# The walk over a strip of eight image columns in the scan's sums into yacc

## The chip, the cores and the metric

The kernel runs on one core of a Trainium2 chip. The metric is the device time of one execution in microseconds (us). Before the change it is 24400.92 us, the median of three runs (24385.79 to 24407.32).

The engines' names in profile lines: PE is TensorE (PEld its weight loads), DVE VectorE, ACT ScalarE, POOL GpSimd, SP SyncE, which here issues DMAs.

## What is computed

Eight images of 64 x 64 pixels and 192 channels go through two layers, each with a residual sum. Layer 0 is a Mamba-2 block between two depthwise convolutions. Layer 1, which the change is in, is a two-dimensional selective scan: four directions run over each image, along rows (k = 0), along columns (k = 1), and both backwards (k = 2 and 3). Their outputs are brought back to the order of rows and summed:

```python
xs = jnp.stack([x_flat, x_t], axis=1)                       # rows, columns
xs = jnp.concatenate([xs, jnp.flip(xs, axis=-1)], axis=1)   # and both backwards
...
dA = jnp.exp(d[..., None] * A[None])
dBu = (d * uu)[..., None] * bm[:, :, None, :]
hst = dA * hst + dBu
y = jnp.einsum('bkdn,bkn->bkd', hst, cm)
...
y = y1 + inv2 + wh + invwh      # wh, invwh: columns, transposed back to rows
```

384 inner channels and 16 states per channel take part. The sum `y` is then normalised over the channels, multiplied with a gate and projected back to 192 channels.

## The kernel before

Layer 0 runs first over all images, then layer 1 image by image. In layer 1 an image has a front stage (projection, depthwise convolution, SiLU; it writes the convolved image to DRAM twice, in the order of rows and in that of columns), a scan stage, and a finishing stage that runs beside the front stage of the next image. Front and finish are ordered by a planner (`Flow`), which takes a weight per step. The scan stage is `main()`, whose order is written out by hand. The sums that the change is in are issued in `main()`, so none of the planner's weights belongs to them.

**The scan.** The 384 channels are three groups of 128 (`d`). One direction of 4096 positions is cut into 8 chunks of 512 (`TT`), so an image has 32 steps `(k, c)`. A step has 24 units: 8 pairs of states (`p`) times 3 groups (`d`). For each unit

- `decay` (L1569, ScalarE) makes exp(delta times A) for 2 x 512 elements,
- `weigh` (L1554, ScalarE) and `supply` (L1580, TensorE transposes) make the inputs of the recurrence in PSUM,
- `run` does two scans of 128 x 512 on VectorE (L1596), one small copy of the last state on GpSimd (L1608) and one product with C on GpSimd (L1610),
- `collect` (L1625, TensorE) sums the states into `y`, a PSUM tile of 128 x 512, one per group `d`; the 8 pairs accumulate into it,
- `add` (L1634 and L1636, VectorE) acts after the eighth pair alone: it adds the finished `y` to `yacc`, the SBUF buffer of 128 x 3 x 4096 in which the four directions meet. For k = 0 it is a copy (L1634), for k = 1, 2 and 3 a sum in place (L1636).

In the loop of `main()` the order on the engines is: `run(u)`, `decay(u + 2)`, some `weigh`, `supply(u + 1)`, `collect(u - 1)`, `add(u - 2)`, then pieces of the preparation of the next step. So the sum of a unit follows two iterations after that unit's `run`: a step's three sums stand in VectorE's queue in three successive iterations (its last one and the first two of the next step), each behind one unit's two scans and ahead of the next unit's. The preparation of a step has some VectorE work of its own (L1446, L1462, L1482, L1502).

**The views.** `yacc` holds each channel's image along rows, position 64 h + w. A chunk of a row direction is 8 rows, that is 512 adjacent words of `yacc`. A chunk of a column direction is 8 adjacent columns of 64 pixels. `y` holds it in the direction's own order, column by column (position 64 w + h within the chunk). `view` picks the chunk's place in `yacc`, and `seq` gives `y` the same order of dimensions. The two lines that matter are `rearrange("p (h w) -> p w h", ...)` in `view`, for yacc, and `rearrange("p (w h) -> p w h", ...)` in `seq`, for y. In both the innermost dimension is h: yacc is walked with a step of 64 words (256 bytes), as source and as destination, and y word after word.

Of the kernel before, what the change touches and what calls it, by code (L numbers as in the profile page):

```python
# [14 lines left out]
NB, HI, WI, C = 8, 64, 64, 192  # L15
# [1014 lines left out]
def layer1(tc, consts, x1s, mv1, out, w_in, w_x, w_dt, w_out):  # L1030
# [7 lines left out]
    with ExitStack() as ctx:  # L1038
# [352 lines left out]
        def view(buf, k, d, at, n):  # L1391

            if k % 2 == 0:
                return buf[:, d, at : at + n]
            return buf[:, d].rearrange("p (h w) -> p w h", w=WI)[:, at // HI : (at + n) // HI, :]

        def seq(ap, k):

            return ap if k % 2 == 0 else ap.rearrange("p (w h) -> p w h", h=HI)

        def scan(xo):

# [224 lines left out]
            def add(u):  # L1627
                s, p, d = units[u]
                k, c = steps[s]
                if p == NP1 - 1:  # L1630
                    ya = view(yacc, k, d, c * TT, TT)
                    yv = seq(state[s]["y", d], k)
                    if k == 0:
                        o(nc.vector.tensor_copy(ya, yv))  # L1634
                    else:
                        o(nc.vector.tensor_add(ya, ya, yv))  # L1636
# [218 lines left out]
```

## Time and profile before

| what | value |
|---|---|
| median of three runs | 24400.92 us |
| the profiled execution's own time | 24391.89 us |
| its span | 24390.1 us |
| TensorE clock granted, mean | 0.973 |
| VectorE busy | 21614.8 us (89%) |
| ScalarE busy | 21445.6 us (88%) |
| TensorE busy | 20962.6 us (86%) |
| GpSimd busy | 16900.2 us (69%) |
| chain of waits, largest shares | GpSimd 53%, TensorE 23% |
| L1634, copies of y into yacc | 192 of 665 ns |
| L1636, sums of y into yacc | 576, 625.5 us busy |

A line of the groups gives line, engine, operation, tiles and shapes, the count, then busy time and mean duration of one in ns, then the engine's idle time before such instructions and what ended it. A line of one source line's view gives the shortest, median and longest duration. A line of a stretch gives its bounds and length in us, then each engine's busy time with its count of instructions, the granted clock, the DMA share and the rate. A line of the timeline gives start, duration, engine, line and operation; a bracket at its end is idle time before it and what ended that.

From 4.8 ms or so on, layer 1 runs; the scans take most of it. Within it, each image's scan stage shows 32 steps of about 67 to 70 us.

### The profile page before, as it was taken

Reading aid. Unit: us, or ns where it says so; the run is one execution under the profiler, and the core shown is the slowest. Engines: PE = TensorE matmul, PEld = TensorE weight load, DVE = VectorE, ACT = ScalarE, POOL = GpSimd, SP = SyncE. Lnnn points to the kernel's source line nnn. Section 1 sums busy time; section 2 is a strip of 40 time slices with the busy share of each in tenths; the row PEclk is TensorE's granted clock in tenths of the full one; section 3 lists DMA queues with packets and bytes.
Section 4 is the critical chain, followed back from the end, with each engine's and each line's share of the span. In section 5 each row is a group of like instructions: output and inputs, shape, how many; then the busy total and the mean of one; then the engine's idle time right before and its main releaser. Section 6 shows DMA issues by size and latency. Waiting matters only on the chain.

```text
span 24390.1 us, 313055 instructions
## 1 busy us (share of the span) xinstructions
PE 20962.6 (86%) x100036; PEld 10175.2 (42%) x100036; DVE 21614.8 (89%) x22093; ACT 21445.6 (88%) x38076; POOL 16900.2 (69%) x13639
## 2 busy tenths in 40 slices
PE   7999999978888888888888888888888888888888
PEld 4444444434443444344434443444344334434444
DVE  7888888689988999899989998999899989998998
ACT  5666666589998999899889998998899899989998
POOL 1111111169976997799779977997799779977997
PEclk8999999989999999999999999999999999999999
DMA  2111111122222222222222222222222222222221
GB/s 49 44 43 45 46 44 46 39 84 66 67 68 85 66 67 70 84 66 67 71 81 67 67 75 79 65 67 74 81 65 67 73 81 67 67 71 81 66 67 56
DMA packets 1129702, 1608.05 MB, mean 66 GB/s; under 512 B 259360, under 2 KB 458432, under 8 KB 1118848
## 3 DMA queue, kind: packets, MB, share of 16 engines
q1 hardware_dynamic: 1128064, 1588.03, 23.0%
q8 instruction: 806, 13.21, 0.2%
q14 instruction: 832, 6.82, 0.1%
HBM read 1024.65 MB, written 160.17 MB: 49 GB/s over the span
## 4 chain that ended last, share of the span: by engine, by line
POOL 53%; PE 23%; issue 9%; DVE 7%; ACT 6%; DMA 1%; SPq 0%; POOLq 0%; DVEq 0%; ACTq 0%
POOL hc L1610 48%; POOL cy L1608 4%; PE p_f L953 3%; DVE xs L1200 2%; PE y L1625 2%; ACT pw L1554 2%; PE p_f L973 2%; ACT ea L1569 2%; PE p_x L445 2%; PE p_o L870 1%; POOL du L1489 1%; PE p_y L787 1%; PE p_z L528 1%; PE p_o L1374 1%; DMA xc<-xo 1%
## 5 line engine op out<-in xcount | busy, mean ns | idle before, releaser
L1610 POOL TENSOR_TENSOR hc<-hs,cb 128x1024 f32<-128x1024 f32 x6144 | 14597.2, 2376 | 9.8 <-POOL cy L1608 5.2
L1596 DVE TENSOR_TENSOR_SCAN hs<-ea,cy,g 128x512 f32<-128x512 f32 x10752 | 13061.1, 1263 | 785.6 <-PE g L1580 412.2
L1554 ACT ACTIVATE pw<-duT,bt 128x384 f32<-128x384 f32 x16384 | 8873.7, 601 | 12.2 <-DVE duT L1502 12.2
L1625 PE MATMUL y<-hc,sel 128*64 128x512 f32 x24576 | 6652.9, 620 | 2470.5 <-POOL hc L1610 2463.7
L1569 ACT ACTIVATE ea<-dr,an 128x512 f32<-128x512 f32 x12288 | 8125.8, 709 | 350.7 <-DVE hs L1596 328.5
L1580 PEld LDWEIGHTS g<-ident,pw 128*128 128x128 f32 x49152 | 5306.7, 141 | 4301.4 <-issue 2670.3
L1580 PE MATMUL g<-ident,pw 128*128 128x128 f32 x49152 | 6771.8, 280 | 30.0 <-DVE hs L1596 12.9
L1625 PEld LDWEIGHTS y<-hc,sel 128*64 128x64 f32 x24576 | 1228.7, 135 | 3889.7 <-POOL hc L1610 3629.3
L1608 POOL COPY cy<-hs 128x2 f32<-128x2 f32 x6144 | 1179.3, 192 | 1543.8 <-DVE hs L1596 1431.3
L1489 POOL TENSOR_TENSOR du<-de,xc 128x512 f32<-128x512 f32 x768 | 984.8, 1282 | 1636.4 <-DVE de L1482 1620.1
L1596 DVE TENSOR_TENSOR_SCAN hs<-ea,g 128x512 f32<-128x512 f32 x1536 | 1777.2, 1205 | 180.6 <-PE g L1580 125.8
L362 POOL TENSOR_TENSOR s<-xs 96x512 f32<-96x512 f32 x64 | 117.0, 1829 | 2035.0 <-DVE xs L340 1523.2
L1200 DVE SCALAR_TENSOR_TENSOR xs<-pad,p,xs 128x4096 f32<-128x4096 f32 x192 | 860.8, 4484 | 37.4 <-ACT xs L1190 30.2
L1468 PE MATMUL p_dt<-xdbl,wd 13*128 13x512 f32 x1536 | 856.8, 639 | 41.6 <-DVE de L1482 39.7
L362 POOL TENSOR_TENSOR s<-sq 96x512 f32<-96x512 f32 x128 | 206.7, 1615 | 965.4 <-ACT sq L375 890.2
L1439 PE MATMUL p_d<-xc,wx 128*44 128x512 f32 x1536 | 792.7, 598 | 96.3 <-DMA xc<-xo 96.3
L340 DVE SCALAR_TENSOR_TENSOR x<-xx,p,x 96x512 f32<-96x512 f32 x1024 | 784.8, 814 | 15.3 <-ACT x L329 15.3
L953 PE MATMUL p_f<-h,wf 96*128 96x512 f32 x1536 | 763.9, 633 | 24.4 <-ACT zs L547 14.0
L340 DVE SCALAR_TENSOR_TENSOR xs<-xin,p,xs 96x512 f32<-96x512 f32 x1024 | 749.8, 768 | 4.6 <-ACT xs L329 4.6
L1482 DVE SCALAR_TENSOR_TENSOR de<-p_dt,spa 128x512 f32<-128x512 f32 x768 | 524.2, 683 | 254.3 <-ACT spa L1477 253.5
L973 PE MATMUL p_f<-m,wf 128*96 128x512 f32 x1536 | 692.1, 601 | 0.0
L1636 DVE TENSOR_TENSOR yacc<-yacc,y 128x512 f32<-128x512 f32 x576 | 625.5, 1086 | 16.6 <-PE y L1625 16.6
(201 smaller groups left out, 19661.2 us busy)
## 6 DMA issues: line engine op xcount, KB each, us to landing
cb<-cd SPq DMA_DIRECT2D x4096, 128.0 KB
dr<-de SPq DMA_DIRECT2D x3072, 128.0 KB
xc<-xo SPq DMA_DIRECT2D x256, 768.0 KB
e<-csd SPq DMA_DIRECT2D x256, 384.0 KB
xl<-x SPq DMA_DIRECT2D x256, 384.0 KB
xo<-xs SPq DMA_DIRECT2D x48, 1024.0 KB
xo<-xt SPq DMA_DIRECT2D x24, 2048.0 KB
xl<-in_x SPq DMA_DIRECT2D x64, 384.0 KB
```

The source lines that it names most:

```text
L340: nc.vector.scalar_tensor_tensor(im(out[:, ct]), tap(ct, j), w[:, ct, j : j + 1], im(out[:, ct]), ALU.mult, ALU.add)
L953: nc.tensor.matmul(ps, wf1[:, ct, mt * 128 : mt * 128 + 128], h[:, ct], start=ct == 0, stop=ct == 1)
L973: nc.tensor.matmul(ps[:CP], wf2[:, kt, ct * CP : ct * CP + CP], m[:, kt], start=kt == 0, stop=kt == 5)
L1200: nc.vector.scalar_tensor_tensor(xs, tap(j), kw[:, d, j : j + 1], xs, ALU.mult, ALU.add)
L1489: o(nc.gpsimd.tensor_mul(st["du", d], st["de", d], st["xc"][:, d]))
L1554: nc.scalar.activation(st["pw", p, j][:, :, i], st["duT"][:, j].rearrange("p (g c) -> p g c", c=64), AF.Copy, scale=st["bt"][:, j, n : n + 1],
L1569: nc.scalar.activation(ea[:, f], state[s]["dr", d][:, f], AF.Exp, scale=an[:, k, p, at : at + 1])
L1580: nc.tensor.transpose(g[:, f, j * 128 : j * 128 + 128], state[s]["pw", p, j][:, 2 * d + f].rearrange("p a b -> p (a b)"), ident,)
L1596: nc.vector.tensor_tensor_scan(rev(h[:, f]), rev(ea[:, f]), rev(g[:, f]), 0.0 if first(s) else state[s - 1]["cy"][:, p, d, f : f + 1], ALU ...
L1608: o(nc.gpsimd.tensor_copy(st["cy"][:, p, d], h[:, :, last]))
L1610: o(nc.gpsimd.tensor_mul(hc, h, bc(st["cb", p], 1, [128, 2, TT])))
L1625: o(nc.tensor.matmul(y[half[f]], sel, hc[:, f], start=p == 0 and k > 0, stop=p == NP1 - 1))
```

## The change

Both views are turned, in the column directions alone: the innermost dimension is now w, of which a chunk has 8. yacc is walked along the rows of the strip, 8 adjacent words in each of 64 rows that lie 64 words apart, as source and destination. y, in PSUM, is read in the matching order: 8 words with a step of 64, then the next h. The same elements meet, each sum is one instruction of 512 elements per partition as before, and the row directions (k = 0 and 2) are untouched. Nothing else in the kernel differs.

```diff
             if k % 2 == 0:
                 return buf[:, d, at : at + n]
-            return buf[:, d].rearrange("p (h w) -> p w h", w=WI)[:, at // HI : (at + n) // HI, :]
+            return buf[:, d].rearrange("p (h w) -> p h w", w=WI)[:, :, at // HI : (at + n) // HI]
 
         def seq(ap, k):
 
-            return ap if k % 2 == 0 else ap.rearrange("p (w h) -> p w h", h=HI)
+            return ap if k % 2 == 0 else ap.rearrange("p (w h) -> p h w", h=HI)
```

## The prediction

> **What bounds the kernel now.** I read the groups of instructions first, for the price of the operation that is edited; then its own line; then stretches of the scan, one chunk long, to see whether that price reaches the end; then the engines' order of work inside such a stretch.
>
> ```profile
> L1596 DVE TENSOR_TENSOR_SCAN hs<-ea,cy,g 128x512 f32<-128x512 f32 x10752 | 13061.1, 1263 | 785.6 <-PE g L1580 412.2
> L1636 DVE TENSOR_TENSOR yacc<-yacc,y 128x512 f32<-128x512 f32 x576 | 625.5, 1086 | 16.6 <-PE y L1625 16.6
> ...
> L1636 DVE TENSOR_TENSOR yacc<-yacc,y x576: 657/1285/1358, 5656.5 to 24254.9; 128x512 f32<-128x512 f32 x192
> ```
>
> The sums into yacc (L1636) have one shape but two prices: 657 ns at least, 1285 ns in the median. Of the 576, 192 belong to direction 2 (rows) and 384 to directions 1 and 3 (columns). Sorted by direction with the Vector engine's timeline they take 662 ns (657 to 667) in direction 2, and 1300 and 1296 ns in directions 1 and 3: mean 1298 ns. Check: 192 x 0.662 + 384 x 1.298 = 625.5 us, the row's busy time. So the edit touches 384 instructions that each cost 0.636 us more than their row twin, 244 us of the Vector engine's time.
>
> Whether those 244 us are time of the kernel is seen by setting directions side by side. One chunk from the start of its first sum to that of the next chunk: lines one and two are direction 2, three and four direction 3. Both run backwards in time, with the same instructions, and differ in the view alone.
>
> ```profile
> core 0: us, PE busy (x) PEld busy (x) DVE busy (x) ACT busy (x) POOL busy (x), PEclk, DMA share, GB/s
> 16002.80:16070.45 67.65, 57.63 (x316) 28.49 (x316) 63.61 (x60) 66.97 (x122) 63.37 (x52) 1.00 0.23 69
> 16070.45:16138.11 67.66, 57.78 (x318) 28.46 (x316) 63.62 (x60) 67.27 (x122) 63.36 (x52) 1.00 0.24 67
> ...
> 16545.70:16615.18 69.48, 57.75 (x317) 28.48 (x316) 65.36 (x61) 67.45 (x122) 63.28 (x52) 1.00 0.22 62
> 16615.18:16684.68 69.50, 57.79 (x318) 28.50 (x316) 65.36 (x60) 67.47 (x122) 63.23 (x52) 1.00 0.25 69
> ```
>
> A row chunk takes 67.65 us and ScalarE (ACT) is busy 67.0 to 67.3 us of it: it is the floor there. A column chunk takes 69.5 us, ScalarE works no more than before and is idle for 2 us, and the Vector engine (DVE) has 1.75 us more to do. The place is seen in the order of its work, first direction 2, then direction 3:
>
> ```profile
> 16002.80 0.66 DVE L1636 TENSOR_TENSOR yacc<-yacc,y 128x512 f32<-128x512 f32 x1
> 16003.38 2.44 DVE L1596 TENSOR_TENSOR_SCAN hs<-ea,cy,g 128x512 f32<-128x512 f32 x2
> 16005.74 0.66 DVE L1636 TENSOR_TENSOR yacc<-yacc,y 128x512 f32<-128x512 f32 x1
> ...
> 16545.70 1.28 DVE L1636 TENSOR_TENSOR yacc<-yacc,y 128x512 f32<-128x512 f32 x1
> 16546.89 2.46 DVE L1596 TENSOR_TENSOR_SCAN hs<-ea,cy,g 128x512 f32<-128x512 f32 x2
> 16549.24 1.31 DVE L1636 TENSOR_TENSOR yacc<-yacc,y 128x512 f32<-128x512 f32 x1
> ```
>
> Around the three sums of a chunk the Vector engine has no idle time; sum to sum is 2.94 us in direction 2 and 3.54 us in direction 3. GpSimd (POOL) waits behind it there:
>
> ```profile
> 16549.41 0.19 POOL L1608 COPY cy<-hs 128x2 f32<-128x2 f32 x1 [0.99 <-DVE hs L1596]
> 16552.97 0.19 POOL L1608 COPY cy<-hs 128x2 f32<-128x2 f32 x1 [1.00 <-DVE hs L1596]
> ```
>
> The same waits are 0.37 to 0.43 us in direction 2. The chain of waits gives GpSimd 53% of the span, but in these microseconds it follows the scans, which stand in the Vector queue behind the sum. So a sum's length is on the path, and a row chunk is a model of what a column chunk becomes if its sums get as short.
>
> [...] One reading stream that hops is shown on ScalarE, by its column copy against a copy of the same size along rows:
>
> ```profile
> L1227 ACT COPY xt<-xs 128x4096 f32<-128x4096 f32 x24 | 176.3, 7346 | 0.3
> L1190 ACT ACTIVATE xs<-pad,p 128x4096 f32<-128x4096 f32 x24 | 91.1, 3794 | 0.2
> ```
>
> 7346 / 4096 = 1.79 ns per element against 0.93[...]. No instruction of this trace hops in PSUM.
>
> **The change part by part.**
> Removed: the hop of yacc, as source and destination, in 384 sums. After it yacc comes in runs of 8 adjacent words, 64 of them, each starting at a multiple of 32 bytes. [...] No row here has runs of 8; nothing hides this, it is priced at 0[...]. [...]
> Added: y, in PSUM, was read in order and is now read with a step of 64 words eight times, then from one word on. This decides. [...] I take 0, and keep both ends.
> Moved: nothing. The count of instructions, their order, the queues, the DMAs and the waits are the same; the sums aren't among the costs of the planner. Nothing new is queued behind them.
> Sum, for a sum of 0.662 us. Starts of first sums over the whole trace give these chunk times: direction 1, 69.55 us mean (56 chunks); direction 2, 67.73 (56); direction 3, 69.57 (48). Gains: 56 x (69.55 - 67.73) = 102 us; the last chunk of direction 1 against the last of direction 2, 8 x (68.74 - 66.99) = 14 us; direction 3, 56 x (69.57 - 67.73) = 103 us (the seventh of each image has no next chunk to prepare; I price it the same). The very last chunk's sums stand beside a Vector engine that waits for TensorE (idle 0.36 and 1.19 us before them), and the mean's matmul waits for the last for 0.3 us: 0.25 x 8 = 2 us. Together 221 us of the 244: 91% of a sum's saving reaches the end. The rest is chunk ends, and ScalarE's floor of 67.3 us, which is late next: below it a shorter sum would buy nothing.
> The profiled execution took 24391.9 us (span 24390.1 and 1.8 around it): 24391.9 - 221 = 24171. It was 9 us below the median of 24400.9, so the forecast in medians is **24180 us**, 0.9% faster. Per microsecond of a sum's length: 221 / 0.636 = 347 us.
>
> **The rivals.**
> *PSUM hops like SBUF.* [...] **24300**. [...] With 0.95 to 1.13 us, 24280 to 24342.
> *The stride only moves over.* [...] about **24400**. [...]
> *Slower.* [...] the Vector queue holds the scans longer than now. It decides from a sum of 1.298 + 49 / 347 = 1.44 us on[...] **24526**. [...]
> *ScalarE keeps the time.* It was busy 67.45 us in column chunks against 67.1 in row chunks; if that stayed, a chunk would take 67.45 + 0.6 = 68.05 us, the 112 chunks would gain 1.5 us each and the whole some 170 us: 24230. Equal counts (122) speak against it; it lies in the range.
>
> **Chances.** Free hop (with the ScalarE variant) 0.46; SBUF-like hop 0.34; moved over 0.12; slower 0.08. By the bound of 0.2% (49 us, about what a measurement of this kernel can tell from no change), the first two are faster: 0.80; the third is within: 0.12; 0.08 slower. The range is the first two: from 24155 (24180 less the 21 us by which the runs before spread, rounded) to 24340, where the SBUF-like case ends.
>
> **What would show it.** The line of L1636 has one price, 0.66 us for all 576, busy 381 us; chunks of directions 1 and 3 take 67.7 us like direction 2; sums follow at 2.94 us; GpSimd's copies wait 0.4 us. If the sums are 0.66 and the chunks are not 67.7, the path is wrong; if they take 1.0 us or more, the price of the PSUM hop is, and the time should follow at 347 us per microsecond.

## The result and the profile after

The changed kernel takes 24180.17 us (median of 5 runs, 24169.79 to 24198.37) where the kernel before takes 24407.32 us (5 runs, 24385.79 to 24414.17): a ratio of 0.9909, 95% interval 0.9895 to 0.9922. That is 227 us, or 0.9% less. The forecast was 24180 us.

The sums' own line of the profile after, and their group:

```profile
L1636 DVE TENSOR_TENSOR yacc<-yacc,y x576: 657/662/689, 5666.8 to 24042.8; 128x512 f32<-128x512 f32 x192
L1636 DVE TENSOR_TENSOR yacc<-yacc,y 128x512 f32<-128x512 f32 x576 | 382.0, 663 | 25.7 <-PE y L1625 25.7
```

There is one price now. 657 to 689 ns covers all three directions, and the busy time has fallen from 625.5 to 382.0 us. By direction the medians are 664, 662 and 662 ns for directions 1, 2 and 3: reading y with a step of 64 words in PSUM (directions 1 and 3) costs nothing that these records show beside the reading in order (direction 2, 662 ns).

Two stretches of direction 3 in the profile after, each one chunk long and beginning 0.28 us ahead of a chunk's first sum:

```profile
core 0: us, PE busy (x) PEld busy (x) DVE busy (x) ACT busy (x) POOL busy (x), PEclk, DMA share, GB/s
16430.84:16498.49 67.65, 57.77 (x318) 28.46 (x317) 63.62 (x60) 67.24 (x122) 63.29 (x52) 1.00 0.23 65
16498.49:16566.15 67.66, 57.80 (x318) 28.48 (x317) 63.63 (x60) 67.27 (x122) 63.34 (x52) 1.00 0.25 70
```

They take what the row chunks took before: 67.65 us, with 63.6 us of VectorE and 67.2 us of ScalarE. The order of work at the head of such a chunk, on VectorE and on GpSimd behind it:

```profile
16431.12 0.67 DVE L1636 TENSOR_TENSOR yacc<-yacc,y 128x512 f32<-128x512 f32 x1
16431.70 2.45 DVE L1596 TENSOR_TENSOR_SCAN hs<-ea,cy,g 128x512 f32<-128x512 f32 x2
16434.06 0.67 DVE L1636 TENSOR_TENSOR yacc<-yacc,y 128x512 f32<-128x512 f32 x1
...
16434.22 0.18 POOL L1608 COPY cy<-hs 128x2 f32<-128x2 f32 x1 [0.39 <-DVE hs L1596]
16437.16 0.19 POOL L1608 COPY cy<-hs 128x2 f32<-128x2 f32 x1 [0.39 <-DVE hs L1596]
```

The sums follow each other at 2.94 us, and GpSimd's copies wait 0.39 us instead of 1 us. The gain reaches the end through VectorE's queue, in which the next scan stands behind the sum: the trace before has hardly an instruction on another engine that waits for a sum itself (three waits, 0.9 us in all). ScalarE shows the same in its idle time. The first line is from the kernel before, from its groups:

```profile
L1569 ACT ACTIVATE ea<-dr,an 128x512 f32<-128x512 f32 x12288 | 8125.8, 709 | 350.7 <-DVE hs L1596 328.5
```

and this is the same group after:

```profile
L1569 ACT ACTIVATE ea<-dr,an 128x512 f32<-128x512 f32 x12288 | 8123.2, 709 | 159.9 <-DVE hs L1596 131.9
```

Its work is the same to 3 us. What it waited for VectorE's scans is down by 197 us.

Where the time went is seen best in the scan stages alone (first to last scan of each image, from the traces), because the rest differs from run to run: in kernels with the same layer 0, the first scan starts 5022 to 5051 us into the execution. The eight scan stages took 17535.9 us before and 17317.5 us after: 218.4 us less. The work between them is the same to a few us. One more trace of the changed kernel (run e7_after_again below) gives 17328.6 us: two traces of one kernel can differ by 11 us here.

### The profile page after: what moved, and what is told of

The parts are those of the page before. It is cut to its first block, busy times and chain, and to the rows that moved or that the text cites. A ratio compares the mean times of both kernels' runs of the same rounds, so it can differ in the third digit from the quotient of the medians.

```text
span 24174.9 us, 313055 instructions
## 1 busy us (share of the span) xinstructions
PE 20986.5 (87%) x100036; PEld 10182.8 (42%) x100036; DVE 21386.3 (88%) x22093; ACT 21415.5 (89%) x38076; POOL 16907.4 (70%) x13639
## 4 chain that ended last, share of the span: by engine, by line
POOL 53%; PE 25%; issue 8%; DVE 6%; ACT 5%; DMA 2%; SPq 1%; POOLq 0%; DVEq 0%; ACTq 0%
POOL hc L1610 47%; POOL cy L1608 4%; PE y L1625 3%; PE p_f L953 3%; DVE xs L1200 3%; PE p_f L973 2%; PE p_x L445 2%; PE g L1580 2%; ACT pw L1554 2%; DMA xc<-xo 2%; PE p_o L870 1%; POOL du L1489 1%; ACT ea L1569 1%; PE p_y L787 1%; PE p_d L1439 1%
## 5 line engine op out<-in xcount | busy, mean ns | idle before, releaser
L1482 DVE SCALAR_TENSOR_TENSOR de<-p_dt,spa 128x512 f32<-128x512 f32 x768 | 524.1, 682 | 254.0 <-ACT spa L1477 253.0
L1495 PEld LDWEIGHTS p_du<-ident,du 128*128 128x128 f32 x3072 | 323.1, 141 | 743.2 <-POOL du L1489 500.3
```

## Experiments

The theory: a stream that hops in SBUF lengthens the sum (1.298 us against 0.662 with two such streams, in the trace before), a stream that reads PSUM with hops does not (0.663 us after), and the time that a sum keeps VectorE from its next scan is time of the kernel, until ScalarE's work is the limit. "Hopping" means that the innermost step is more than one word. Each run is compared within itself: chunks of directions 1 and 3 against those of direction 2, which no run alters except where it is said. All runs start from the changed kernel.

**One hopping stream at a time.** The first kernel hops in the source alone, the second in the destination alone.

```diff
-                        o(nc.vector.tensor_add(ya, ya, yv))
+                        src = yacc[:, (d + 1) % DT].rearrange("p (h w) -> p w h", w=WI)[:, 8 * c : 8 * c + 8, :]
+                        dst = yacc[:, d, c * TT : c * TT + TT].rearrange("p (w h) -> p w h", h=HI)
+                        o(nc.vector.tensor_add(dst, src, state[s]["y", d].rearrange("p (w h) -> p w h", h=HI)))
```

(k = 2 keeps its sum; the second kernel exchanges the two views.)

> Leaves out the right place: in directions 1 and 3 the sum reads yacc down the columns of one channel group (step of 64 words) and writes 512 adjacent words of another, y is read in order; the output isn't the reference's. Theory ([...] PSUM has nothing to do with it): [...] at 347 us per us of a sum's length the kernel takes about 24300 us, half-way between after and before. Rival A (only hopping writes are dear, reads hop for nothing): 0.66 us and 24180. Rival B (only hopping reads are dear): 1.30 us and 24400.

> The mirror of the run with the hopping source: in directions 1 and 3 the sum reads 512 adjacent words of yacc in another channel group and writes down the columns (step of 64 words), y is read in order; the output isn't the reference's. Theory (both streams pay by themselves): 1.00 us per sum and about 24300 us. Rival A (only writes are dear): 1.30 us and 24400. Rival B (only reads are dear): 0.66 us and 24180.

Measured: 24298.77 us (ratio to before 0.9963, 0.9951 to 0.9976) with the hopping source and 24256.15 us (0.9951, 0.9938 to 0.9963) with the hopping destination. The sums take 1048 and 1053 ns: both streams pay, and rivals A and B fall. The times lie on either side of the half-way that had been expected of both (a ratio of 0.9955), the second kernel's 44 us below the 24300 named for it; the intervals of the two overlap, so it is their chunks that tell them apart. Equal durations gave unequal chunks. Timeline of VectorE in direction 3, source hopping:

```profile
16491.57 1.05 DVE L1640 TENSOR_TENSOR yacc<-yacc,y 128x512 f32<-128x512 f32 x1
16492.53 2.45 DVE L1596 TENSOR_TENSOR_SCAN hs<-ea,cy,g 128x512 f32<-128x512 f32 x2
16494.89 1.06 DVE L1640 TENSOR_TENSOR yacc<-yacc,y 128x512 f32<-128x512 f32 x1
```

and destination hopping:

```profile
16492.58 1.07 DVE L1640 TENSOR_TENSOR yacc<-yacc,y 128x512 f32<-128x512 f32 x1
16493.47 2.44 DVE L1596 TENSOR_TENSOR_SCAN hs<-ea,cy,g 128x512 f32<-128x512 f32 x2
16495.81 1.05 DVE L1640 TENSOR_TENSOR yacc<-yacc,y 128x512 f32<-128x512 f32 x1
```

Read the starts, not the durations. A sum of 1.06 us holds the next scan back for 0.96 us if it reads with hops, and for 0.89 us if only its writes hop: it then overlaps its successor by 0.17 us and not 0.09 us. So the price of an instruction in a full queue is the time from its start to the next one's. Medians over all sums, against the chunk's excess over row chunks of the same run:

| run | hops in | duration, us | start to next start, us | 3 x its excess over 0.579 | chunk's excess, directions 1 and 3 |
|---|---|---|---|---|---|
| after | PSUM | 0.663 | 0.579 | 0.00 | -0.03, 0.00 |
| destination | SBUF write | 1.053 | 0.884 | 0.92 | 0.84, 0.86 |
| source | SBUF read | 1.048 | 0.965 | 1.16 | 1.11, 1.15 |
| before | SBUF read and write | 1.298 | 1.202 | 1.87 | 1.83, 1.85 |

92 to 99% of the start-to-start excess is found again in the chunk. In the last row, where reads and writes both hop, the overlap is 0.10 us, so the longer overlap belongs to the sum that hops in its writes alone. Why it does wasn't looked into.

**No sums.** The same place in the code with the sum left out for k = 1 and 3:

```diff
-                    else:
+                    elif k == 2:
                         o(nc.vector.tensor_add(ya, ya, yv))
```

> Leaves out the 384 sums of the column directions, so two directions are missing from the output. Theory (below the row sum's price ScalarE's busy time is the floor: 67.3 us of a chunk of 67.65): a column chunk falls by 0.35 us at most, some 40 us in all, to about 24140. Rival (the Vector engine stays the bound around the sums whatever their length): each sum that goes takes 0.58 us with it, 3 x 0.58 x 128 = 223 us, 23960.

Measured: 24111.48 us, 0.9888 (0.9873 to 0.9903) of before. A column chunk and a row chunk of this run:

```profile
15352.03:15419.38 67.35, 58.34 (x318) 28.44 (x317) 62.03 (x57) 67.16 (x122) 63.29 (x51) 1.00 0.25 68
15960.00:16027.70 67.70, 59.05 (x317) 29.00 (x316) 63.38 (x60) 67.32 (x121) 63.41 (x51) 0.97 0.24 67
```

67.35 us, with ScalarE busy 67.16 us of it: taking away 1.74 us (3 x 0.58) of VectorE's queue buys 0.36 us. The eight scan stages are 17295.5 us, 22 and 33 us less than in the two traces of the changed kernel, where some 40 us had been expected at most. The floor is where the theory put it, and the rival falls: from a row sum's price down, the path is no longer VectorE's alone.

**Other steps in PSUM, other engine.** First, all directions read y in PSUM with steps of their own (2, 16, 128 and 256 words) and write 512 adjacent words.

```diff
+                    n = (2, 16, 128, 256)[k]
+                    ya = yacc[:, d, c * TT : c * TT + TT].rearrange("p (a b) -> p a b", b=TT // n)
+                    yv = state[s]["y", d].rearrange("p (b a) -> p a b", b=TT // n)
```

> Every direction takes its chunk of yacc as 512 adjacent words, and reads y with another inner step in PSUM: 2 words in the copies of direction 0, 16, 128 and 256 words in the sums of directions 1, 2 and 3; the elements that meet are the wrong ones, so the output isn't the reference's. Theory (a hopping read of PSUM is free for the Vector engine, whatever the step): 0.66 to 0.67 us each and a time like after, 24180. Rival (free by the luck of the step of 64 words[...]): the step of 16 words takes 1.0 to 1.4 us and direction 1's chunks 69 to 70 us.

Measured: copies of 669 ns (step 2), sums of 665, 666 and 667 ns (steps 16, 128, 256), chunks of 67.63 to 67.65 us in directions 1 to 3, 24181.0 us in one run. Near steps are as free as far ones, though this kernel was timed once.

Then ScalarE, whose operation on 512 words of PSUM read in order is shorter than VectorE's sum (575 ns against 662), reads PSUM with hops:

```diff
-                    o(nc.scalar.activation(a, st["p_dt", d], AF.Abs))
+                    hop = st["p_dt", d].rearrange("p (b a) -> p a b", b=8)
+                    o(nc.scalar.activation(a.rearrange("p (a b) -> p a b", b=8), hop, AF.Abs))
```

> From after: ScalarE's Abs of the softplus (line 1475) reads its PSUM tile with an inner step of 64 words, 8 at a time, and writes 512 adjacent words, so the step sizes go to wrong positions and the output isn't the reference's. It asks for a PSUM word more often than the Vector engine does: the reading in order takes 576 ns for 512. Theory [...]: 576 ns as before. Rival ([...] hidden behind the Vector engine's rate alone): 600 to 680 ns. Rival (ScalarE reads PSUM hops at SBUF's pace[...]): 1000 ns, and the time rises.

The line's durations (shortest, median, longest) in the profile after, then in a second trace of that same kernel (run e7_after_again), then in this run, where the line has become L1476:

```profile
L1475 ACT ACTIVATE spa<-p_dt x768: 568/575/598, 5030.7 to 23950.4; 128x512 f32<-128x512 f32 x192
```

```profile
L1475 ACT ACTIVATE spa<-p_dt x768: 572/582/649, 5006.3 to 23942.4; 128x512 f32<-128x512 f32 x192
```

```profile
L1476 ACT ACTIVATE spa<-p_dt x768: 571/582/645, 5028.2 to 23959.8; 128x512 f32<-128x512 f32 x192
```

582 ns with hops, and 575 or 582 ns without, depending on the trace: the hops cost nothing that can be seen, where SBUF's price on this engine (1.79 against 0.93 ns per element, L1227 and L1190 in the profile before) would have added some 440 ns by our estimate ((1.79 - 0.93) x 512). The 7 ns lie between two traces of one kernel, and so are no price of hops; the logarithm and exponential of the same step, which hop nowhere, move with them from 630 to 632 ns.

**Short runs in SBUF.** The sums walk yacc in runs of 1, 2 and 4 words.

```diff
+                    n = (512, 1, 2, 4)[k]
+                    yv = state[s]["y", d].rearrange("p (a b) -> p a b", b=n)
...
+                        ya = yacc[:, d].rearrange("p (a b) -> p a b", b=8 * n)[:, :, c % (8 // n) * n :][:, :, :n]
+                        o(nc.vector.tensor_add(ya, ya, yv))
```

> The sums walk yacc, as source and destination, in runs of 1, 2 and 4 adjacent words (directions 1, 2 and 3) with a step of 8, 16 and 32 words between runs; y is read in order. The places are wrong ones, so the output isn't the reference's. Theory (a pair of adjacent words pays for the hop): 1.2 to 1.4 us for runs of one word, 0.66 us for runs of two and of four. Rival (a run has to be longer to hide the hop): the runs of two take 0.8 to 1.0 us, those of four about 0.7 to 0.8.

Timeline of VectorE in this run, one sum of direction 1 (runs of one word) and one of direction 2 (pairs), each with the scan after it:

```profile
15444.20 1.10 DVE L1637 TENSOR_TENSOR yacc<-yacc,y 128x512 f32<-128x512 f32 x1
15445.20 1.27 DVE L1596 TENSOR_TENSOR_SCAN hs<-ea,cy,g 128x512 f32<-128x512 f32 x1
...
15993.80 0.67 DVE L1637 TENSOR_TENSOR yacc<-yacc,y 128x512 f32<-128x512 f32 x1
15994.38 2.45 DVE L1596 TENSOR_TENSOR_SCAN hs<-ea,cy,g 128x512 f32<-128x512 f32 x2
```

Runs of one word take 1.10 us, less than the 1.2 to 1.4 us that had been expected; runs of two take 0.665 us and of four 0.667 us. The kernel took 24250.0 us in its one run. In this run a pair pays for the hop (0.665 us against 0.662 in order), so the change's runs of 8 (0.663 us) had room to spare. A step of 8 words is cheaper (start to next start 1.00 us) than one of 64 (1.20 us), and again the chunks follow: 3 x (1.002 - 0.579) = 1.27 us, measured 1.24 us over direction 2's chunks, whose runs of two words cost nothing.

**Is ScalarE the limit now?** The changed kernel was run once more (24178.83 us, 0.9913, 0.9899 to 0.9926; scan stages 17328.6 us where 17317 had been expected) beside one that makes 3 of a chunk's 64 scalings on VectorE:

```diff
+                if p in (4, 5, 6) and j == 1 and i == 0:
+                    o(
+                        nc.vector.tensor_scalar_mul(
+                            st["pw", p, j][:, :, i],
+                            st["duT"][:, j].rearrange("p (g c) -> p g c", c=64),
+                            st["bt"][:, j, n : n + 1],
+                        )
+                    )
+                    return
```

> The changed kernel as it is, beside the next run on the same chip. Theory: scan stages of 17317 us in all, sums of 0.66 us, 0.991 of the kernel before.

> From after, computing the same: 3 of the 64 ScalarE scalings of a chunk (line 1554) are made on the Vector engine, in the middle of a chunk where its sums do not stand. Theory (ScalarE's busy time, 67.0 to 67.3 us of a chunk of 67.65, is what limits a chunk now): ScalarE is freed of 3 x 0.60 = 1.8 us, the Vector engine gets 3 x 0.4 = 1.2 us and still has idle time; chunks fall by about 1 us to 66.6, and the kernel by some 250 us to about 23930. Rival (the Vector engine is the limit, with the sums or without): chunks grow by up to 1.2 us, about 24400 us.

Measured: 24174.89 us, 0.9906 (0.9892 to 0.9920): no different from after. ScalarE's group and VectorE's in this run, then VectorE's line by shortest, median and longest duration:

```profile
L1563 ACT ACTIVATE pw<-duT,bt 128x384 f32<-128x384 f32 x15616 | 8517.3, 606 | 14.1 <-DVE duT L1502 14.1
L1555 DVE TENSOR_SCALAR pw<-duT,bt 128x384 f32<-128x384 f32 x768 | 513.8, 669 | 0.0
...
L1555 DVE TENSOR_SCALAR pw<-duT,bt x768: 392/398/1426, 5053.0 to 24000.4; 128x384 f32<-128x384 f32 x192
```

The mean of 669 ns hides two prices. In the median, two of a chunk's three scalings take the 0.40 us that had been expected, and the one between them takes 1.2 us. The timeline shows what is different, first a short one, then a long one, each with GpSimd's product next to it:

```profile
12605.07 0.39 DVE L1555 TENSOR_SCALAR pw<-duT,bt 128x384 f32<-128x384 f32 x1
12605.47 2.35 POOL L1619 TENSOR_TENSOR hc<-hs,cb 128x1024 f32<-128x1024 f32 x1
...
12612.32 2.37 POOL L1619 TENSOR_TENSOR hc<-hs,cb 128x1024 f32<-128x1024 f32 x1
12613.70 1.20 DVE L1555 TENSOR_SCALAR pw<-duT,bt 128x384 f32<-128x384 f32 x1
```

The short one is over when a product starts; the long one starts inside a product and ends 0.21 us after it. All 768 fall in these two kinds. The 299 scalings that started more than 0.15 us ahead of a running product's end took 0.47 to 1.43 us, and each ended 0.21 to 0.27 us after that product; the 469 others took 0.39 to 0.40 us. In this run such a scaling is held up by the product that it meets. So VectorE took on 2.0 us per chunk for ScalarE's 1.8, and ScalarE's waits for VectorE's scans ahead of its exponentials grew from 125.5 us (e7_after_again) to 358.4 us. Neither the theory's 250 us nor the rival's loss came, and the run doesn't tell which engine was the limit. The next two leave work out and add none:

```diff
                     o(nc.scalar.activation(a, a, AF.Exp, scale=-1.0))
-                    o(nc.scalar.activation(a, a, AF.Ln, bias=1.0))
```

> From after, leaves out ScalarE's logarithm of the softplus (line 1477, 3 x 0.63 us of a chunk): the step sizes are somewhat too large, so the output isn't the reference's. It frees ScalarE and loads no other engine, which the run with the moved scalings did not do. Theory (ScalarE is what limits a chunk now, busy 2052 of 2070 us): a chunk of directions 1 to 3 falls from 67.66 us by 1 to 1.8 us, to about 66.2, and the scan stages by 250 to 450 us. Rival (scan, product and matmul pass a unit round among the engines, and this round is the limit; ScalarE's 99% is only the result): chunks stay within 0.3 us of 67.66.

> From the run without the logarithm, leaves out the 384 column sums as well, so two directions are missing and the step sizes are too large. Theory (with ScalarE freed, the Vector engine's sums lie on the path again, at their start-to-start price): column chunks are 3 x 0.58 = 1.7 us shorter than the row chunks of the same run, or as much as ScalarE's new floor (65.5 us) lets. Rival (the sums are hidden elsewhere): column and row chunks differ by 0.3 us, as they do with the logarithm in place.

Measured: 24036.9 us (0.9862, 0.9847 to 0.9876) and 23950.05 us (0.9824, 0.9808 to 0.9841). A row chunk without the logarithm:

```profile
15821.49:15888.65 67.16, 57.54 (x319) 28.54 (x318) 63.40 (x61) 65.86 (x118) 63.30 (x51) 1.00 0.25 68
```

and a column chunk without logarithm and sums:

```profile
15233.08:15299.23 66.15, 57.48 (x319) 28.55 (x318) 62.05 (x58) 65.71 (x119) 62.99 (x51) 1.00 0.25 69
```

Freed of 1.9 us, ScalarE gives back 0.5 us of the chunk (67.66 to 67.16) and then has 1.3 us of idle time: half of the least that the theory asked for, and more than the rival allowed. In that kernel the sums are worth 1.0 us per chunk (67.17 against 66.15), less than the 1.7 us that had been expected, where they were worth 0.36 us with the logarithm in place. We read this as two limits that stand close together in a chunk after the change: VectorE at its head, where the sums are, and ScalarE elsewhere. But leaving out the logarithm does a second thing: VectorE's step that uses the softplus (L1482 after the change) had waited 253.0 us for it in all, and waits 19.0 us without the logarithm. How much of the 0.5 us comes from that, and how much from ScalarE's freed time, these runs don't part. Shortening the one alone buys 0.36 us, the other alone 0.5 us, both together 1.5 us. "ScalarE is the floor" is true for a shorter sum, and is not the whole of a chunk. What holds the remaining idle time of both engines wasn't isolated.

## Why the prediction was right

**The price of the new sum** was the open step: the hop in PSUM was taken at 0, at a chance of 0.46. The trace before priced no hop in PSUM, and its sums hop in two SBUF streams at once (1.298 us against 0.662), so the 0 and the price of one SBUF-like hop in VectorE's sum were the author's estimates. Measured: 0.663 us for 0.662. Four other steps on VectorE (0.665 to 0.669 us) and ScalarE's shorter operation (582 ns with hops, 575 to 582 without) show no price either; how fast PSUM can be read was not measured. The rival "PSUM hops like SBUF" lost on the price alone, its path was right: the kernel that does hop in one SBUF source needs 135 to 146 us more in its scan stages than the changed one (17463.1 against 17328.6 and 17317.5), where the rival's 24300 us lay 120 us over the forecast.

**Yacc in runs of 8 at 0:** this too was the author's estimate, as the trace before priced no such runs. Measured 0 (0.663 us against 0.662 in order), and runs of 2 would have done (0.665 us).

**That a sum's length is on the path:** right. Sums came at 2.94 us, chunks at 67.63 and 67.65 us, GpSimd's waits at 0.39 us, as listed ahead of the run.

**The sum of the gains:** forecast 102 + 14 + 103 + 2 = 221 us in the profiled execution. The scan stages gained 218.4 us: 103 for direction 1, 14 for its last chunks, 102 for direction 3, and nothing for the last chunk of an image, which had been given 2 us. The profiled executions differ by 215 us (24391.9 against 24176.65), the medians by 227 us. That the forecast of 24180 us and the median after agree to less than a microsecond is luck: the five runs after spread over 29 us, and the median before moved by 6 us when it was taken again.

**What was loose:** the rate of 347 us per us counted a sum by its duration (0.636 us of excess). The queue loses by start to next start (0.623 us), and for a hopping write the two part. By duration (0.385 and 0.390 us of excess) the rate gives the source-hopping and the destination-hopping kernel 134 and 135 us over the changed one; their scan stages show 135 to 146 us and 104 to 115 us (17463.1 and 17432.4 against 17328.6 and 17317.5). So it is the hopping write that the rate misses. "91% reaches the end" is in these terms nearly all of it where a chunk has a successor; what is lost is the last chunk of each image. One reading was loose too: the ScalarE line that the column copy was set beside (L1190) scales and adds a bias along padded rows, and is no plain copy.

**ScalarE as next limit:** right for shorter sums (0.36 us per chunk when they go), too simple as a statement on the chunk. ScalarE's variant of the forecast (24230) did not come: its busy time in column chunks fell from 67.45 to 67.25 us when the waits fell.

## What to carry to other kernels

When a VectorE sum on fp32 has to transpose between an SBUF operand and a PSUM input, give the PSUM side the hops and the SBUF side runs of two adjacent words or more: the sums of 128 x 512 here took 0.663 us with PSUM hopping and SBUF in runs of 8 words, 0.665 and 0.667 us with PSUM in order and runs of 2 and 4, 1.05 us with one SBUF stream hopping by 64 words and 1.30 us with two (the runs measured here start at multiples of 8 bytes). Where one code path serves several directions or cases, the case that doesn't have the suspected cost is a measured model of the change: set its stage beside the dear one before estimating anything. Price an instruction in a full queue by the time to its successor's start (a sum recorded at 0.663 us held the next scan back by 0.579 us). When one line has a mean far from its median (1086 and 1285 ns for the sums before), look for two prices in it. Expect a gain to end where another engine's busy time nearly fills the stage (with ScalarE busy for 67.2 of 67.65 us, 1.74 us less of VectorE's queue bought 0.36 us).

## What the runs showed of the hardware

A VectorE sum of 128 x 512 elements costs the same with its PSUM input read in order (0.662 us) and with steps of 16 to 256 words (0.66 to 0.67 us), and a copy with a step of 2 takes 0.67 us; ScalarE's read of 128 x 512 takes 582 ns with hops and 575 to 582 ns without. By start to start, beyond the sum with SBUF read and written in order or in runs (0.579 us), a step of 64 words in SBUF costs 0.75 ns per element on a reading stream (0.386 us of 512), 0.60 ns on the writing one (0.305), and 1.22 ns on both (0.623), a little less than their sum; a step of 8 words on both costs 0.83 ns (0.423). A sum whose writes alone hop lets the next instruction start earlier within its recorded duration: 0.17 us before its end instead of 0.085; with hops in reads and writes it is 0.10. VectorE's scaling of 128 x 384 fp32 elements from SBUF to SBUF took 0.39 to 0.40 us where it met no running GpSimd product of 128 x 1024, or its last 0.15 us at most; where it started earlier inside one it ended 0.21 to 0.27 us after the product's end, 1.2 us long in most cases.
